# Gathered blocks as one run of 17 tiles, and one block multiplied with its counts as stationary operand

## The chip, the cores and the metric

The kernel runs on one core of one Trainium2 chip. The metric is the device time of one launch in microseconds, as the median over runs. One further execution was profiled; all rows of the profile come from it.

## The reference

Four layers of a graph network over 6250 nodes of 256 channels and 100,000 edges, sorted by destination (`N`, `C`, `E`; `NOUT` is 64):

```python
def agg(h):
    return jax.ops.segment_sum(h[src], dst, num_segments=N)
x = jnp.maximum(_layernorm(x_in), 0.0)
for l in range(3):
    h = x + agg(x)
    h = relu(h @ W1s[l] + b1s[l])
    h = relu(h @ W2s[l] + b2s[l])
    x = h @ W3s[l] + b3s[l]
h = x + agg(x)
h = relu(h @ cW1 + cb1)
h = relu(h @ cW2 + cb2)
return x_in + h @ cW3 + cb3
```

Edges are drawn at random: a block of 128 destination nodes has about 2050 of them.

## The kernel before, in words

The 6250 nodes are 49 blocks of 128. The first matrix of each layer is applied ahead of the aggregation, so a layer's table holds rows that only have to be summed. A table stands in DRAM (`tables`) and, split into a high and a low half, in SBUF (`XY`, 512 columns for each of 49 source blocks).

A block's sum over its edges is made in one of two ways.

- **Dense, in panels.** In layer 0 a matrix of edge counts is built for some blocks by matmuls of one-hot matrices (`build`, lines 1016 to 1056; its one-hots `hi` and `lo` come from VectorE, line 997) and stored as bytes in DRAM (`mats`). A panel is up to four such blocks. For each of 49 source blocks (a *unit*), the counts are cast to a ring tile `a` (`prepare`, lines 1500 and 1502), and four matmuls with `XY` as stationary operand and the counts as moving operand add to two PSUM tiles (`product`, line 1527). The result has channels on partitions, as the following layers of the network want it.
- **Gathered.** Rows of the table are fetched by indirect DMAs on GpSimd, 128 rows of 1 KB each (`Gathered.send`, line 1345, a *gather*), and added by matmuls with one-hot matrices (`one_hots`, line 1370; `add`, line 1389), 32 destination nodes to one quarter of PSUM's partitions. The result has nodes on partitions; it is turned by transposes (line 1427).

Before the change 18 blocks are gathered (22 in layer 0, where the panel of blocks 44 to 47 isn't built in time), in 18 tiles each: nine for each half of the block (`TS = 9`, `T = 18`). The other 31 (27) are dense: seven panels of four blocks and one, the first, of three (blocks 17 to 19).

The order of instructions on each engine is written out by the program. `tick` counts units, and jobs are put between them; a model clock (`passed`, with the costs of line 1456) says how far PE should be. A gathered block is added in two *visits*, each to a part of its tiles, between two units; `meets` says when. `flow` sends gathers evenly over a layer, `LEAD` (21 us on the model clock) ahead of their visit. A gather waits for the matmul behind which it was sent (`after`), and for a free buffer (24 in layer 0, 26 later). A layer's gathers begin when the whole table of the layer before is stored (`begin`). The second and third product of each group of blocks (`mlp`, lines 1198 and 1255; in the last layer 1190 and 1210) follow some units later.

Layer 0 is opened by `PRE` ticks, in which counts are built and no product runs: all steps of the first panel and eight more, two a tick. The preparation ahead of it (`look`, `normed`) finds where each block's edges begin, fetches them, makes the gather indices `idx` and each edge's destination in its block (`rel`), and judges whether the edges fit the tiles (`wrong`); where they don't, a second program (`any_edges`) does all again.

Of the kernel before, what the change touches and what calls it, by code (L numbers as in the profile page):

```python
# [8 lines left out]
F32 = mybir.dt.float32  # L9
# [8 lines left out]
P = 128  # L18
# [378 lines left out]
def sorted_edges(  # L397
# [57 lines left out]
    TS = 9  # L455
    T = 2 * TS
    CUT = (3, 5)

    ROUNDS = [(3, 3), (4, 4), (0, 5), (1, 6), (2, 7), (None, 8)]
# [10 lines left out]
    gone = [(0, 4), (4, 4), (8, 4), (12, 4), (16, 1), (44, 4), (48, 1)]  # L470
    panels = [(17, 3), (20, 4), (24, 4), (28, 4), (32, 4), (36, 4), (40, 4), (44, 4)]
    S0 = 2 * panels[0][0]
    assert gone[-2] == panels[-1] and sorted(
# [16 lines left out]
    rel = const.tile([P, left[NQ]], F32, name="rel")  # L490
# [4 lines left out]
    wrong = const.tile([P, 4], F32, name="wrong")  # L495
# [4 lines left out]
    mats = [dram.tile([P, NT // CH, n, CH * P], U8, name=f"mat{p}") for p, (_, n) in enumerate(panels)]  # L500
# [108 lines left out]
    def look(pool):  # L609
# [23 lines left out]
        nc.vector.memset(one, 1.0)  # L633
        firsts = pool.tile([1, EB], F32, name="near", bufs=1)
# [26 lines left out]
        for q, (b, _) in enumerate(gone):  # L661
            nc.gpsimd.iota(place_i[:, q, :], pattern=[[1, PW]], base=T * b, channel_multiplier=-TS)
        place = pool.tile([P, 1], F32, name="place", bufs=1)
# [29 lines left out]
        for q in range(GSUB):  # L693
            for w, e in ((wd, dst), (ws, src)):
# [4 lines left out]
        both = pool.tile([P, 2], F32, name="both", bufs=1)  # L699
        sel = pool.tile([P, NQ, PW], F32, name="near_i", bufs=1)  # L700
        some = pool.tile([P, NQ, PW], F32, name="rel", bufs=1)
        nc.vector.tensor_copy(both[:NSUB, 0:1], first[:NSUB, 0:1])
        nc.vector.tensor_copy(both[:NSUB, 1:2], low[:NSUB])
        nc.vector.tensor_scalar(some[:NSUB], place_i[:NSUB], float(TS - 1), None, op0=OP.is_le)
        nc.vector.scalar_tensor_tensor(sel[:NSUB], place_i[:NSUB], 0.0, some[:NSUB],
                                       op0=OP.is_ge, op1=OP.mult)
        ps = ps_m.tile([P, W], F32, name="ps")
        for q in range(NQ):
            nc.tensor.matmul(ps[:PW, 2 * q:2 * q + 2], sel[:NSUB, q, :], both[:NSUB, :],
                             start=True, stop=True)  # L710
        spread = pool.tile([P, NQ, 2], F32, name="spread", bufs=1)
        nc.vector.tensor_copy(spread[:PW], ps[:PW, :2 * NQ].rearrange("p (q t) -> p q t", t=2))
# [25 lines left out]
        for q0 in range(0, GSUB, H):  # L738
# [42 lines left out]
        nc.vector.tensor_scalar(size[:NSUB, 0:1], less[:NSUB, GSUB:], less[:NSUB, 0:1],  # L781
                                float(TS * P), op0=OP.subtract, op1=OP.is_gt)
        nc.vector.tensor_scalar(size[:NSUB, 1:2], less[:NSUB, Q // GD:Q // GD + 1],
                                less[:NSUB, 0:1], float(CUT[1] * P), op0=OP.subtract, op1=OP.is_gt)
        nc.vector.tensor_scalar(size[:NSUB, 2:3], less[:NSUB, Q // GD:Q // GD + 1],
                                less[:NSUB, 0:1], float(CUT[0] * P), op0=OP.subtract, op1=OP.is_lt)
        nc.vector.tensor_reduce(wrong[:NSUB, 3:4], size[:NSUB, 0:3], axis=mybir.AxisListType.X,
                                op=OP.max)
# [10 lines left out]
        for t, o in ((fd, rel), (fs, idx)):  # L799
            ps = ps_m.tile([P, W], F32, name="ps")  # L800
            for q, (_, n) in enumerate(gone):
                nc.tensor.transpose(ps[:, left[q]:left[q + 1]], t[:n * T, q, :],
                                    ident[:n * T, :n * T])
            if o is rel:
                nc.vector.tensor_scalar(o, ps[:, :left[NQ]], -1.0, None, op0=OP.add)
            else:
                nc.vector.tensor_copy(o, ps[:, :left[NQ]])
# [3 lines left out]
    def verdict():  # L811
        bad = ps_m.tile([P, W], F32, name="ps")
        nc.tensor.matmul(bad[:1, :4], one, wrong, start=True, stop=True)
        return bad

    def judge(bad):
        nc.vector.tensor_reduce(amiss, bad[:1, :4], axis=mybir.AxisListType.X, op=OP.add)
# [108 lines left out]
    with tc.manual_schedule():  # L926
# [38 lines left out]
        def load_weights(l):  # L965
# [4 lines left out]
            else:  # L970
                w3 = late.tile([2 * NOUT, C], F32, name="cw3", bufs=1)
                for h in range(2):
                    nc.sync.dma_start(out=w3[h * NOUT:(h + 1) * NOUT, :], in_=cW3)
                row = late.tile([P, C], F32, name="cb3r", bufs=1)
# [6 lines left out]
        batches = [(p, s, q0) for p, (b0, n) in enumerate(panels)  # L981
# [34 lines left out]
        def build(hots, ats, ps_b):  # L1016
# [7 lines left out]
            for k, (p, s, q0) in enumerate(batches):  # L1024
                i, half = divmod(s - 2 * panels[p][0], 2)
# [5 lines left out]
                for q in range(0, BATCH, 2):  # L1031
# [17 lines left out]
                    if half and q0 + q + 2 == GSUB:  # L1049
                        own = at[:, panels[p][0] + i, :]  # L1050
# [9 lines left out]
        def first_chunks(i, at):  # L1060

            n = panels[0][1]
            if i == n - 1:
                for k, chunk in enumerate(opening):
# [3 lines left out]
                        chunk[:, :n, j * P:(j + 1) * P] for j in range(CH))  # L1068
# [8 lines left out]
        def fetch(l, p):  # L1077

            n = panels[p][1]
            c = len(mat.setdefault((l, p), [])) // CH  # L1080
            at = chunks.tile([P, 4, CH * P], U8, name="at", bufs=5)
            nc.sync.dma_start(out=at[:, :n, :], in_=mats[p][:, c, :, :])
            mat[l, p].extend(at[:, :n, j * P:(j + 1) * P] for j in range(CH))
# [216 lines left out]
        class Gathered:  # L1300
            def __init__(self, l):
# [4 lines left out]
                               if l == 0 or (b, n) != panels[-1]]  # L1306
                self.alone = {b + i for b, n, i, _ in self.blocks}
                self.visits = [(g, rounds) for g in range(len(self.blocks)) for rounds in VISITS[l > 0]]
# [3 lines left out]
                self.order = [(g, k, h) for g, rounds in self.visits for k in self.tiles(rounds)  # L1312
                              for h in range(2)]
                self.upto = [0]
                for _, rounds in self.visits:
                    self.upto.append(self.upto[-1] + 2 * len(self.tiles(rounds)))

            @staticmethod
            def tiles(rounds):
                return sorted({k for r in rounds for k in ROUNDS[r] if k is not None})  # L1320
# [18 lines left out]
            def send(self, upto):  # L1339
                while self.sent < min(upto, len(self.order)):  # L1340
                    g, k, h = self.order[self.sent]
                    t = gath.tile([P, C], F32, name="rows")
                    self.rows[g, h, k] = t
                    o = self.blocks[g][3] + h * TS + k
# [16 lines left out]
            def one_hots(self, v):  # L1361
                g, rounds = self.visits[v]
                o = self.blocks[g][3]
                self.hots = {}
                for r in rounds:
                    hot = work.tile([P, 2, 2, Q], F32, name="hot", bufs=6)
                    for i, k in enumerate(ROUNDS[r]):
                        if k is not None:
                            self.hots[r, i] = hot[:, i, :, :]
                            nc.vector.tensor_tensor(  # L1370
                                hot[:, i, :, :],
                                colf[:, None, i * Q:(i + 1) * Q].to_broadcast([P, 2, Q]),
                                rel[:, o + k:o + k + TS + 1:TS, None].to_broadcast([P, 2, Q]),
                                OP.is_equal)

            def add(self):
# [3 lines left out]
                if rounds[0] == 0:  # L1380
                    self.sums = sums
                if v == 0:
                    self.one_hots(0)
                end = rounds[-1] == len(ROUNDS) - 1
                for r in rounds:
                    for h in range(2):
                        for m, k in enumerate(ROUNDS[r]):
                            if k is not None:
                                nc.tensor.matmul(  # L1389
                                    self.sums[(2 * h + m) * Q:(2 * h + m + 1) * Q, :C],  # L1390
                                    self.hots[r, m][:, h, :], self.rows[g, h, k], start=(r == 0),
# [264 lines left out]
```

## Time and profile before

| | us |
|---|---|
| median of 3 runs | 2163.5 (2163.37 to 2166.09) |
| the profiled execution: time | 2161.71 |
| the profiled execution: span | 2159.9 |
| mean granted clock of TensorE | 0.991 |

| engine | busy us | share of the span |
|---|---|---|
| PE, matmuls | 2102.0 | 97% |
| VectorE (DVE) | 987.4 | 46% |
| ScalarE (ACT) | 900.7 | 42% |
| GpSimd (POOL) | 1417.2 | 66% |

How to read it: the times of all rows are microseconds from the start of the span, except where "mean ns of one" is said. A matmul in fp32 is recorded as two instructions, one in fp32r (the products of line 1527) or bf16 (line 1038) as one. Busy time of PE is the union of its instructions' modelled spans. Layer 0 runs to about 722 us, layers 1, 2 and 3 begin there, at 1215 and at 1709.

### The profile page before, as it was taken

Reading aid. Unit: us, or ns where it says so; the run is one execution under the profiler, and the core shown is the slowest. Engines: PE = TensorE matmul, PEld = TensorE weight load, DVE = VectorE, ACT = ScalarE, POOL = GpSimd, SP = SyncE. Lnnn points to the kernel's source line nnn. Section 1 sums busy time; section 2 is a strip of 40 time slices with the busy share of each in tenths; the row PEclk is TensorE's granted clock in tenths of the full one; section 3 lists DMA queues with packets and bytes.
Section 4 is the critical chain, followed back from the end, with each engine's and each line's share of the span. In section 5 each row is a group of like instructions: output and inputs, shape, how many; then the busy total and the mean of one; then the engine's idle time right before and its main releaser. Section 6 shows DMA issues by size and latency. Waiting matters only on the chain.

```text
span 2159.9 us, 34383 instructions
## 1 busy us (share of the span) xinstructions
PE 2102.0 (97%) x12106; PEld 1553.3 (72%) x12106; DVE 987.4 (46%) x2844; ACT 900.7 (42%) x1816; POOL 1417.2 (66%) x1442
## 2 busy tenths in 40 slices
PE   5889999999999999999999999999999999999998
PEld 4657766766666877777777877777777877777775
DVE  7988666666664532222234433322333433333323
ACT  4876655556555423233324433232223433333331
POOL 3637777777775366666666366666666277777773
PEclk9979999999999999999999999999999999999999
DMA  5556656656565655544555655545555565556563
GB/s 162 167 162 198 189 177 188 188 184 195 168 212 180 199 158 154 162 142 148 157 169 178 193 159 155 160 138 163 155 171 170 158 202 183 188 168 193 191 191 110
DMA packets 195965, 371.51 MB, mean 172 GB/s; under 512 B 32808, under 2 KB 123068, under 8 KB 195782
## 3 DMA queue, kind: packets, MB, share of 16 engines
q0 software_dynamic: 67264, 181.96, 28.6%
q1 hardware_dynamic: 126590, 185.40, 26.1%
q8 instruction: 97, 1.59, 0.3%
q10 hardware_dynamic: 1928, 1.85, 0.3%
q14 instruction: 86, 0.70, 0.1%
HBM read 310.67 MB, written 58.07 MB: 171 GB/s over the span
## 4 chain that ended last, share of the span: by engine, by line
PE 91%; DVE 4%; ACT 2%; DMA 2%; issue 1%; POOL 0%; SPq 0%; ACTq 0%; DVEq 0%; POOLq 0%
PE agg L1527 62%; PE sums L1389 10%; PE ps L1198 6%; PE ps L1255 6%; PE bp L1038 4%; DVE hi L997 1%; PE ps L1427 1%; DMA back<-table 1%; PE bp L882 1%; PE ps L1210 1%; DVE lo L997 0%; PE ps L1190 0%; PE ps L578 0%; ACT at L1046 0%; DMA table<-zs 0%
## 5 line engine op out<-in xcount | busy, mean ns | idle before, releaser
L1345 POOL DMA_INDIRECT rows<-table,idx x1368 | 1362.7, 996 | 668.3 <-PE agg L1527 267.4
L1527 PE MATMUL agg<-a,XY 128*128 128x512 f32 (+1 forms) x6076 | 1455.3, 391 | 5.9 <-ACT h L1543 2.9
L1527 PEld LDWEIGHTS agg<-a,XY 128*128 128x128 f32 x6076 | 1105.2, 188 | 259.8 <-issue 51.2
L1500 ACT CAST a<-at 128x512 fp32r<-128x512 uint8 (+1 forms) x943 | 554.8, 607 | 606.1 <-PE agg L1527 581.1
L1502 DVE CAST a<-at 128x512 fp32r<-128x512 uint8 (+1 forms) x576 | 270.9, 474 | 529.0 <-PE agg L1527 496.8
L1389 PE MATMUL sums<-rows,hot 128*32 128x256 f32 x3344 | 231.3, 384 | 2.6 <-DMA rows<-table,idx 1.9
L1046 ACT CAST at<-bp 128x392 uint8<-128x392 f32 x276 | 131.0, 488 | 215.1 <-PE bp L1038 212.7
L1048 DVE CAST at<-bp 128x392 uint8<-128x392 f32 x220 | 123.8, 563 | 157.6 <-PE bp L1038 157.2
L1389 PEld LDWEIGHTS sums<-rows,hot 128*32 128x32 f32 x3344 | 103.3, 109 | 117.4 <-issue 50.6
L1038 PE MATMUL bp<-hi,lo 128*128 128x196 bf16 x992 | 133.8, 259 | 10.4 <-DVE hi L997 9.0
L1416 DVE TENSOR_TENSOR u<-u,sums 128x256 f32<-128x256 f32 x76 | 31.7, 418 | 240.6 <-PE agg L1527 240.6
L997 DVE TENSOR_TENSOR hi<-cols,pairs 128x784 bf16<-128x784 bf16 x248 | 138.3, 558 | 0.0
L1198 PE MATMUL ps<-h,w 128*128 128x512 f32 (+4 forms) x348 | 136.8, 536 | 0.0
L1255 PE MATMUL ps<-w,h 128*128 128x256 f32 x588 | 133.7, 379 | 0.0
L1038 PEld LDWEIGHTS <-lo 128*128 128x128 bf16 x992 | 73.9, 100 | 81.7 <-DVE hi L997 33.4
L1370 DVE TENSOR_TENSOR hot<-colf,rel 128x64 f32<-128x64 f32 x836 | 126.4, 216 | 0.0
L1255 PEld LDWEIGHTS ps<-w,h 128*128 128x128 f32 x588 | 110.9, 190 | 15.3
L997 DVE TENSOR_TENSOR lo<-lanes,pairs 128x512 bf16<-128x512 bf16 x248 | 103.1, 416 | 2.1 <-ACT pairs L992 1.3
L1263 DVE TENSOR_TENSOR zz<-ps,w 128x512 f32<-128x512 f32 (+1 forms) x78 | 50.4, 657 | 117.1 <-PE ps L1255 117.1
L1198 PEld LDWEIGHTS ps<-h,w 128*128 128x128 f32 (+1 forms) x348 | 62.6, 191 | 53.8 <-issue 44.3
L1201 ACT ACTIVATE h<-ps,bias 128x512 f32<-128x512 f32 (+4 forms) x87 | 53.2, 628 | 98.3 <-PE ps L1198 98.2
L1434 ACT ACTIVATE h<-ps,bias 128x256 f32<-128x256 f32 (+1 forms) x84 | 33.5, 450 | 133.2 <-PE ps L1427 133.1
(143 smaller groups left out, 743.2 us busy)
## 6 DMA issues: line engine op xcount, KB each, us to landing
at<-mat SPq DMA_DIRECT2D x189, 448.0 KB
mat<-at SPq DMA_DIRECT2D x31, 784.0 KB
rows<-table,idx POOLq DMA_INDIRECT x1368
table<-zz SPq DMA_DIRECT2D x69, 256.0 KB
back<-table SPq DMA_DIRECT2D x118, 128.0 KB
at<-mat SPq DMA_DIRECT2D x25, 336.0 KB
xs<-in_x_dram SPq DMA_DIRECT2D x8, 768.0 KB
table<-zs SPq DMA_DIRECT2D x24, 256.0 KB
```

Of the source, the lines that this page charges most:

```text
L997: nc.vector.tensor_tensor(o.rearrange("p q (n t) -> p q n t", t=2), values.rearrange("p (n t) -> p n t", t=2)[:, None, :, :].to_broadcast( ...
L1038: mm = nc.tensor.matmul(bp[:, m * HW:(m + 1) * HW], lo[:, q + m, :], hi[:, q + m, :], start=True, stop=True)
L1046: nc.scalar.copy(o, v)
L1048: nc.vector.tensor_copy(o, v)
L1198: mm = nc.tensor.matmul(ps[:mp, :w], weights[l][0][:, c, i * P:i * P + mp], h1[:, c, :w], start=(c == 0), stop=(c == KC - 1))
L1255: mm = nc.tensor.matmul(o, h2[0][:, c, nodes], w3[:, c, :], start=(c == 0), stop=(c == KC - 1))
L1345: got = nc.gpsimd.indirect_dma_start(out=t, out_offset=None, in_=tables[self.l][:, :], in_offset=bass.IndirectOffsetOnAxis(ap=idx[:, o:o + ...
L1370: nc.vector.tensor_tensor(hot[:, i, :, :], colf[:, None, i * Q:(i + 1) * Q].to_broadcast([P, 2, Q]), rel[:, o + k:o + k + TS + 1:TS, None] ...
L1389: nc.tensor.matmul(self.sums[(2 * h + m) * Q:(2 * h + m + 1) * Q, :C], self.hots[r, m][:, h, :], self.rows[g, h, k], start=(r == 0), stop= ...
L1500: nc.scalar.copy(o, mat[l, p][j])
L1502: nc.vector.tensor_copy(o, mat[l, p][j])
L1527: mm = nc.tensor.matmul(agg[c][:, :w], XY[:, j, o:o + P], a[:, :w], start=(j == 0 and half == 0), stop=(j == NT - 1 and half == 1))
```

## The change

A gathered block becomes one run of 17 tiles (`T = 17`), without halves. Quarter m of the block's nodes may have its edges in tiles 4m - 1 to 4m + 4, and the matmuls go in rounds of one tile for each quarter, 23 in place of 22. The one-hots of a visit are made by one VectorE operation of 128x384, in place of five or six of 128x64. Where the quarters' edges must end is judged by four bounds (`CUTS`).

Blocks 16 to 18 are now gathered in each layer: 20 blocks (25 in layer 0, block 19 among them). Block 19 is `solo` in layers 1 to 3: its counts are built and stored as before, but multiplied as the stationary operand, with 512 columns of `XY` as moving operand, 49 matmuls in place of a share of panel matmuls; the sum of its two halves is then turned together with block 18. It comes after three panels. Seven panels of four blocks are left (six in layer 0), and counts are built for 29 blocks in place of 31. The opening has 36 ticks in place of 28, since the first panel has four blocks. The last layer's small tiles are put where the build's inputs were, and the later gather pool has 27 buffers.

The core of the diff:

```diff
-    TS = 9
-    T = 2 * TS
-    CUT = (3, 5)
-
-    ROUNDS = [(3, 3), (4, 4), (0, 5), (1, 6), (2, 7), (None, 8)]
+    T = 17
+    CUTS = ((3, 5), (7, 9), (11, 13), (0, T))
+    ROUNDS = ((3, 1, -1), (0, 4, 2))
...
-    gone = [(0, 4), (4, 4), (8, 4), (12, 4), (16, 1), (44, 4), (48, 1)]
-    panels = [(17, 3), (20, 4), (24, 4), (28, 4), (32, 4), (36, 4), (40, 4), (44, 4)]
+    gone = [(0, 4), (4, 4), (8, 4), (12, 4), (16, 4), (44, 4), (48, 1)]
+    panels = [(20, 4), (24, 4), (28, 4), (32, 4), (36, 4), (40, 4), (44, 4)]
+    solo = (19, 1)
+    stock = panels + [solo]
...
             def one_hots(self, v):
                 g, rounds = self.visits[v]
...
-                for r in rounds:
-                    hot = work.tile([P, 2, 2, Q], F32, name="hot", bufs=6)
-                    for i, k in enumerate(ROUNDS[r]):
-                        if k is not None:
-                            self.hots[r, i] = hot[:, i, :, :]
-                            nc.vector.tensor_tensor(
...
+                shape = [P, len(rounds), P // Q, Q]
+                self.hot = work.tile(shape, F32, name="hot", bufs=2)
+                nc.vector.tensor_tensor(
+                    self.hot,
+                    colf.rearrange("p (m q) -> p m q", q=Q)[:, None, :, :].to_broadcast(shape),
+                    rel[:, self.blocks[g][3] // T, v % len(ROUNDS), :, :, None].to_broadcast(shape),
+                    OP.is_equal)
...
+                for c in rounds:
+                    for m in range(P // Q):
+                        if c + 4 * m >= 0:
+                            nc.tensor.matmul(
+                                self.sums[m * Q:(m + 1) * Q, :C],
+                                self.hot[:, (c - min(rounds)) // 2, m, :], self.rows[g, c + 4 * m],
+                                start=(c == ROUNDS[0][0]), stop=(c == ROUNDS[-1][-1]))
...
+        def product_by_node(l, ps_a):
+            agg = ps_a.tile([P, W], F32, name="agg")
+            for j0, m in solo_parts:
+                u = now[0]
+                tick(layers[l])
+                layers[l].advance()
+                prepare(u + 1 + AHEAD + 2)
+                a = ring.pop(u)
+                for j in range(j0, j0 + m):
+                    mm = nc.tensor.matmul(agg, a[:, (j - j0) * P:(j - j0 + 1) * P], XY[:, j, :],
+                                          start=(j == 0), stop=(j == NT - 1))
+                    passed(W * COLS, mm)
+            u = spare[:, :C]
+
+            def halves():
+                nc.scalar.copy(u, agg[:, :C])
+                later(1, lambda: nc.vector.tensor_tensor(u, u, agg[:, C:], OP.add))
+
+            later(1, halves)
+            alone[l] = u
...
-        gath = ctx.enter_context(tc.tile_pool(name="gath2", bufs=26))
+        gath = ctx.enter_context(tc.tile_pool(name="gath2", bufs=27))
```

More of the change, by code (lines that the diff above doesn't have):

```diff
@@ L1379, in add @@
                 b, n, i, _ = self.blocks[g]
-                if rounds[0] == 0:
-                    self.sums = sums
+                self.sums = sums
                 if v == 0:
                     self.one_hots(0)
[L1384 to L1391, printed above, removed]
-                                    stop=(r == (len(ROUNDS) - 2 if m == 0 else len(ROUNDS) - 1)))
+                end = rounds == ROUNDS[-1]
+                for c in rounds:
+                    for m in range(P // Q):
[4 more added lines that the diff above has]
+                                start=(c == ROUNDS[0][0]), stop=(c == ROUNDS[-1][-1]))
                 passed(VISIT)
@@ L1458, in sorted_edges @@
         FAR, SPAN = 7, 6
-        ends = [PRE + NT * sum(k + 1 for k in last[:l + 1]) for l in range(NLAYER + 1)]
-        VISITS = [[[0, 1, 2], [3, 4, 5]], [[0, 1, 2], [3, 4, 5]]]
+        ends = [sum(1 for k, *_ in units if k <= l) for l in range(NLAYER + 1)]
         layers = [Gathered(l) for l in range(NLAYER + 1)]
@@ L1465, in work_of @@
         def work_of(l):
-            t = sum(n for _, n in panels[:last[l] + 1]) * P * NT * 2 * KC * COLS
-            t += len(layers[l].blocks) * (sum(VISIT for _ in VISITS[l > 0]) + TURN)
+            t = sum(stock[p][1] for p in order[l]) * P * NT * 2 * KC * COLS
+            t += len(layers[l].blocks) * (len(ROUNDS) * VISIT + TURN)
             for k, n in ((l, NT - panels[last[l]][1]), (l - 1, panels[-1][1])):
@@ L1547, in sorted_edges @@
         load_weights(0)
-        total = GSUB * sum(n for _, n in panels)
+        total = GSUB * sum(n for _, n in stock)
         built, goals = [0], []
```

173 lines of the change are left out of this document (106 added, 67 removed).

## The prediction

> **What bounds the kernel now.** I read the page first: its engine shares, then its chain of waits.
>
> ```profile
> PE 2102.0 (97%) x12106; PEld 1553.3 (72%) x12106; DVE 987.4 (46%) x2844; ACT 900.7 (42%) x1816; POOL 1417.2 (66%) x1442
> ...
> PE 91%; DVE 4%; ACT 2%; DMA 2%; issue 1%; POOL 0%; SPq 0%; ACTq 0%; DVEq 0%; POOLq 0%
> ```
>
> By these rows PE is the bound and POOL has a third of its time free. The change takes work from PE and gives some to POOL, so I looked at POOL's gathers alone: the groups by line in three stretches, inside layer 0 (160 to 650 us), layer 1 (740 to 1180) and layer 3 (1740 to 2130). After the bar stand busy us and mean ns of one, then the idle time before them.
>
> ```profile
> L1345 POOL DMA_INDIRECT rows<-table,idx x355 | 369.9, 1042 | 120.9 <-issue 61.9 <-PE bp L1038 29.3 <-PE agg L1527 23.8
> ...
> L1345 POOL DMA_INDIRECT rows<-table,idx x309 | 299.7, 970 | 141.4 <-PE agg L1527 86.2 <-issue 36.6 <-PE ps L1255 9.4
> ...
> L1345 POOL DMA_INDIRECT rows<-table,idx x302 | 298.4, 988 | 93.2 <-issue 46.6 <-PE agg L1527 39.2 <-DMA rows<-table,idx 3.7
> ```
>
> The timeline shows POOL at both ends of layer 3, and PE's last visit (a visit is one of the two halves in which a gathered block is summed):
>
> ```profile
> 1712.88 0.95 POOL L1345 DMA_INDIRECT rows<-table,idx  x1 [33.74 <-DMA cw<-in_L_gnn_cW_dram]
> ...
> 2128.03 0.96 POOL L1345 DMA_INDIRECT rows<-table,idx  x1 [0.30 <-issue]
> ...
> 2131.03 0.95 POOL L1345 DMA_INDIRECT rows<-table,idx  x1 [0.30 <-DMA rows<-table,idx]
> ...
> 2132.80 1.60 PE L1389 MATMUL sums<-rows,hot 128*32 128x256 f32 x20
> ```
>
> In layer 3 a gather takes 298.4 / 302 = 0.988 us and is preceded by 93.2 / 302 = 0.309 us of idle time. The 0.30 stands even before a gather that waits for nothing ("issue"), so it is part of the price: 1.297 us each, and POOL never rests there. The page counts that 0.30 as idle, which is how a saturated engine shows 66%. The last gather ends at 2131.98 and the visit that needs it starts 0.8 us later. So layer 3 already has two bounds of one length. In layer 0 a gather costs 1.042 + 0.30 = 1.342 against a spacing of (369.9 + 120.9) / 355 = 1.383: 3% of slack. At that layer's end it is gone, and PE stands until rows land:
>
> ```profile
> 685.44 0.95 POOL L1345 DMA_INDIRECT rows<-table,idx  x1 [0.30 <-DMA rows<-table,idx]
> ...
> 688.24 0.62 PE L1389 MATMUL sums<-rows,hot 128*32 128x256 f32 x2 [0.66 <-DMA rows<-table,idx]
> ```
>
> Layer 1 has room: 0.970 + 0.30 = 1.270 against (299.7 + 141.4) / 309 = 1.427; layer 2 is built like it.
>
> The Trainium skill, Perfetto Trace Analysis, section GPSIMD Engine Instruction, advises timing this engine by start-to-start spacing, not by reported spans. That is what the sum of the two columns does.
>
> **PE's part.** Prices come from the chain of waits in undisturbed stretches, and from the groups by form.
>
> ```profile
> 1215.21 21.50 PE agg L1527 x124
> ...
> 798.48 12.03 PE agg L1527 x52
> 810.51 1.43 PE sums L1389 x20
> ...
> 947.49 3.43 PE ps L1198 x8
> 950.92 1.43 PE sums L1389 x24
> ...
> 963.96 3.45 PE ps L1255 x16
> ```
> ```profile
> L1038 PE MATMUL bp<-hi,lo 128*128 128x196 bf16 x992 | 133.8, 259 | 10.4 <-DVE hi L997 9.0 <-ACT at L1046 0.6
> ...
> L1427 PE MATMUL ps<-ident,u 128*128 128x128 f32 x152 | 23.5, 272 | 0.6 <-DVE zz L1239 0.6
> ```
>
> Removed in each of four layers: the panel of three blocks, 196 matmuls 384 wide at 21.50 / 124 = 0.173, 34.0 us. Added in layers 1 to 3: the solo block, 49 matmuls 512 wide at 12.03 / 52 = 0.231, 11.3 us. No row shows counts as stationary operand; the shape is that of the 512-wide products, and a doubled price (22.7) is the other end. Added: three gathered blocks in layer 0, two in each other layer. A block has 23 matmuls (46 recorded) instead of 22, still in two visits; visits of 20 and of 24 recorded ones both take 1.43, so a block costs 2.86, plus two transposes of 23.5 / 152 = 0.155: 3.2 us. Builds fall from 31 blocks to 29: 64 matmuls of 133.8 / 992 = 0.135, 8.6 us, all in layer 0.
>
> The opening, which builds the first panel's counts before any product, grows from 56 steps to 72. Its window:
>
> ```profile
> 118.30:145.10 26.80, 19.92 (x114) 10.64 (x113) 24.44 (x59) 23.57 (x61) 8.69 (x8) 0.66 0.54 170
> ```
>
> Columns are length, then busy us of PE, PEld, DVE, ACT and POOL. It runs at DVE's pace (24.44 of 26.80), so 16 steps more cost 16 × 26.80 / 56 = 7.7 us. The new preparation has some ten small DVE operations more near its end; I give them 1 us.
>
> PE alone: layer 0, -34.0 + 9.6 - 8.6 + 7.7 + 1 = -24; layers 1 to 3, -34.0 + 11.3 + 6.4 + 0.3 (the solo's transposes) = -16.0 each. Together -72.
>
> **POOL's part.** Gathers go from 396 to 425 in layer 0 and from 324 to 340 in the others: 1445 against 1368. Each waits in POOL's order, and the visit behind it holds PE's whole queue, so late rows stop the dense products too. Asking earlier does not help an engine that never rests.
>
> Layer 0: of 425 gathers the planner places 12 in the opening (8 before). The first gather behind it was here:
>
> ```profile
> 147.47 0.95 POOL L1345 DMA_INDIRECT rows<-table,idx  x1 [18.34 <-PE agg L1527]
> ```
>
> It moves by 8.7 us to 156.2. Then 413 × 1.342 = 554 us: the last ends at 710, against 686.4. PE alone would finish this layer at about 689 - 24 = 665, so rows set the end: +24 us.
>
> Layers 1 and 2 run from first gather to last visit:
>
> ```profile
> 727.02 0.95 POOL L1345 DMA_INDIRECT rows<-table,idx  x1 [40.62 <-DMA at<-mat]
> ...
> 1219.05 0.95 POOL L1345 DMA_INDIRECT rows<-table,idx  x1 [32.15 <-DMA w<-in_L_gnn_W2s_dram]
> ```
> ```profile
> 1191.33 1.50 PE L1389 MATMUL sums<-rows,hot 128*32 128x256 f32 x20
> ```
>
> That is 464.3 us. The cycle of 492 loses 16.0 on PE; of its rest, about 8 us of PE work moves behind the last visit, where four blocks (16 to 19) must now pass the second and third product instead of one (3.43 + 3.45, less a quarter of that) and the next layer's first products are 512 wide. The stretch becomes 464 - 24 = 440, and POOL needs 340 × 1.270 = 432, or 441 at layer 3's 1.297. The two meet; I take -15 a layer.
>
> Layer 3: 340 × 1.297 = 441, plus 1 until the last visit, against 2132.80 - 1712.88 = 419.9: +22, where PE alone would have 396. The tail behind it loses about 1. The step from layer 0 to 1 gains 2 (its first products are wider).
>
> **At nothing** stand the edits that other work hides.
>
> ```profile
> L1500 ACT CAST a<-at 128x512 fp32r<-128x512 uint8 (+1 forms) x943 | 554.8, 607 | 606.1 <-PE agg L1527 581.1
> ...
> DMA packets 195965, 371.51 MB, mean 172 GB/s; under 512 B 32808, under 2 KB 123068, under 8 KB 195782
> ...
> at<-mat SPq DMA_DIRECT2D x25, 336.0 KB
> ```
>
> ACT's 943 casts for the products fall to 830; it waits for PE in nearly all the idle time ahead of them, so fewer bring nothing. The solo's sum leaves PSUM by one ACT copy and one DVE addition in each of three layers; block 18, which takes it along into the transposes, ends more than half a layer later. If that cover failed, it would be about 1 us a layer. On SP's queue the 28 chunk loads of the narrow panel go and six of the solo's come; with 77 more gathers of 131 KB, and two blocks fewer to build and store, the 371 MB stay within 1%. The last layer's two small weight loads go to a tile that the builds have left free; SP issues them at the same place. The longer order of one-hots per visit is DVE's, and DVE has half its time free behind the opening.
>
> **Sum.** +24 + 2 - 15 - 15 + 22 - 1 = +17 us. The profiled execution has a span of 2159.9 and a time of 2161.7; 2161.7 + 17 = 2178.7. The median of the three runs, 2163.5, is 1.8 above it, which would make 2180.5; I forecast 2179.
>
> **What is unknown** is a gather's price. In layer 0 it swells beside DVE operations that read two SBUF tiles:
>
> ```profile
> 670.47 0.41 DVE L1407 TENSOR_TENSOR u<-XY 128x256 f32<-128x256 f32 x1
> 670.54 1.99 POOL L1345 DMA_INDIRECT rows<-table,idx  x1 [0.30 <-issue]
> 670.81 0.41 DVE L997 TENSOR_TENSOR lo<-lanes,pairs 128x512 bf16<-128x512 bf16 x1
> 671.14 0.55 DVE L997 TENSOR_TENSOR hi<-cols,pairs 128x784 bf16<-128x784 bf16 x1
> ...
> L997 DVE TENSOR_TENSOR hi<-cols,pairs 128x784 bf16<-128x784 bf16 x201 | 112.1, 558 | 0.0
> ...
> L1370 DVE TENSOR_TENSOR hot<-colf,rel 128x64 f32<-128x64 f32 x836 | 126.4, 216 | 0.0
> ```
>
> The change makes the one-hots of a block (11 of 216 ns) into two wide ones, 128x384, whose duration I put between the 216 and the 558 ns of these rows' kinds. They read the same two tiles as the old ones (`rel` now in bf16), so I count no new stall. The other end: layer 0's surplus over layer 1, 355 × (1.042 - 0.970) = 25.6 us, charged to the 201 one-hots `hi` in that stretch, is 0.13 us each; 90 such in layers 0 and 3 are +12, and 80 in layers 1 and 2 +10. Low end: half the surplus of layer 0 (-15) and layer 1's 1.270 in layer 3 (-9).
>
> The Trainium skill, SBUF — State Buffer, section Who interferes with whom, infers that a tensor_tensor does not stall descriptor generation, while a cast in a two-port mode does. In layer 0 only ACT makes the casts `a<-at`, and gathers are longest there, beside tensor_tensors; the trace speaks against the inference. By that rule the wide one-hots would add 0, as in my sum.
>
> **The rivals.** First, PE stays the bound and the kernel gets faster: -72, so 2163.5 - 72 = 2091. It needs the 0.30 before each gather to vanish with demand; it decides below about (665 - 157 - 2) / 413 = 1.22 us a gather in layer 0 and 395 / 340 = 1.16 in layer 3. For it: PE's 97%. Against: 302 gathers in a row at 1.297. Chance 0.07. The Trainium skill, DMA: Bandwidth & Descriptors, section Anatomy of one DMA, calls descriptor generation small until many are emitted; by that rule the extra gathers are nearly free and this rival holds. The rows above deny it.
>
> Second, the wide one-hots stall gathers as `hi` does: +22 on the forecast, 2201. For it: the 1.99 us gather. Chance 0.14.
>
> Third, gain and loss cancel: POOL's price falls by 17 / 753 = 0.023 us over layers 0 and 3, because fewer builds disturb it; 2163. Chance 0.10.
>
> Fourth, the kernel's own verdict finds a block beyond 17 tiles, and the second program runs as well: its some 829 gathers in each of four layers at 1.25 are over 4,100 us more. Counted over the reference's destinations, the fullest gathered block has 2130 edges, 17 tiles hold 2176, and the quarter marks lie inside their bounds. Chance 0.01.
>
> **How the numbers follow.** The forecast has 0.68. The range takes the low end of the price, 2179 - 24, rounded down for the solo and the boundaries, and the high end with 5 us beyond: 2152 to 2206; it leaves out the first and the fourth rival. 0.2% (4.3 us) is about what a measurement of this kernel can tell from no change. Faster by more: the first rival and a third of the third, 0.10; within: 0.07; slower: 0.83.
>
> **What would show it.** Right: in the profile after, layers 0 and 3 have gathers with 0.30 idle before nearly each, PE idle ahead of `sums` put down to DMA rows, some 45 us in layer 0 and 45 in layer 3, and PE's share down to about 93%; the last gather of layer 0 near 710. The solo's 147 products take 34 us. Wrong: a spacing of gathers below 1.22 us in layer 0, or visits that never wait while the time falls.

## The result, and the profile after

The changed kernel took 2179.1 us (median of four runs, 2175.6 to 2180.9) against 2164.0 before: 1.0066 times as long, 95% interval 1.0049 to 1.0083. Forecast were 2179 and "slower". The profiled execution has a span of 2179.1 us, 19.2 more than before, while the medians are 15.1 apart: a profile is one execution, and can lie some us off the median.

The first view is again the page's engine shares (busy us, share of the span, instructions).

```profile
PE 2068.1 (95%) x11971; PEld 1467.6 (67%) x11971; DVE 907.2 (42%) x2108; ACT 843.8 (39%) x1682; POOL 1492.8 (69%) x1521
```

PE has 34 us less to do and the span is 19 us longer. POOL still looks a third idle. The groups by line say why that is wrong; they are the gathers of the same three stretches as in the prediction (160 to 650 us, 740 to 1180, 1740 to 2130).

```profile
L1377 POOL DMA_INDIRECT rows<-table,idx x368 | 370.3, 1006 | 120.7 <-issue 60.3 <-PE bp L1068 25.2 <-PE agg L1586 22.3
...
L1377 POOL DMA_INDIRECT rows<-table,idx x328 | 324.0, 988 | 144.8 <-issue 59.1 <-DMA back<-table 43.4 <-PE agg L1586 33.8
...
L1377 POOL DMA_INDIRECT rows<-table,idx x303 | 298.7, 986 | 92.4 <-issue 49.4 <-PE agg L1586 29.9 <-DMA rows<-table,idx 8.5
```

In layer 3 a gather has 92.4 / 303 = 0.305 us of idle time ahead of it. In layer 1 it has (144.8 - 43.4) / 327 = 0.310, once the 43.4 us before the layer's first gather are left out; it was 0.458 before. So POOL now runs without a rest in layer 1 too. In layer 0 the mean, 0.328, still holds the opening. The timeline shows where each layer's gathers begin, and the last ones.

```profile
137.17 1.05 POOL L1377 DMA_INDIRECT rows<-table,idx  x1 [0.30 <-issue]
151.74 1.35 POOL L1377 DMA_INDIRECT rows<-table,idx  x1 [13.52 <-PE bp L1068]
...
165.75 0.95 POOL L1377 DMA_INDIRECT rows<-table,idx  x1 [2.71 <-PE agg L1586]
...
710.76 0.95 POOL L1377 DMA_INDIRECT rows<-table,idx  x1 [0.30 <-issue]
...
755.06 1.44 POOL L1377 DMA_INDIRECT rows<-table,idx  x1 [43.36 <-DMA back<-table]
...
1234.49 1.03 POOL L1377 DMA_INDIRECT rows<-table,idx  x1 [38.62 <-PE agg L1586]
...
1714.38 1.02 POOL L1377 DMA_INDIRECT rows<-table,idx  x1 [38.48 <-PE agg L1586]
...
2152.39 0.95 POOL L1377 DMA_INDIRECT rows<-table,idx  x1 [0.30 <-issue]
```

Layer 0's last gather starts at 710.8; "near 710" was forecast. Cut at the first gather of each layer, the two spans compare like this:

| us | before | after | difference | forecast |
|---|---|---|---|---|
| start to layer 1's first gather | 727.0 | 755.1 | +28.0 | +26 |
| to layer 2's | 492.0 | 479.4 | -12.6 | -15 |
| to layer 3's | 493.8 | 479.9 | -13.9 | -15 |
| to the end | 447.0 | 464.7 | +17.7 | +21 |

What PE lost is in the row of its visits, in layers 0, 1 and 3 (160 to 715 us, 755 to 1200, 1714 to 2160):

```profile
L1414 PE MATMUL sums<-rows,hot 128*32 128x256 f32 x1150 | 93.2, 394 | 29.4 <-DMA rows<-table,idx 28.5 <-DVE hot L1397 0.6 <-DVE u L1441 0.3
...
L1414 PE MATMUL sums<-rows,hot 128*32 128x256 f32 x920 | 60.7, 383 | 0.8 <-DMA rows<-table,idx 0.8
...
L1414 PE MATMUL sums<-rows,hot 128*32 128x256 f32 x920 | 77.6, 387 | 22.3 <-DMA rows<-table,idx 21.9
```

Idle time tells only half of it. The 920 visit matmuls of layer 3 are "busy" for 77.6 us and the same 920 of layer 1 for 60.7: part of the wait for rows is drawn as busy time inside a visit. So layer 3 loses 22.3 + 16.9 = 39 us to rows. Layer 0 loses 29.4 + (93.2 - 60.7 x 1150 / 920) = 47. The visits show it one by one (start, duration, idle time before):

```profile
711.10 1.08 PE L1414 MATMUL sums<-rows,hot 128*32 128x256 f32 x8 [2.00 <-DMA rows<-table,idx]
713.58 1.91 PE L1414 MATMUL sums<-rows,hot 128*32 128x256 f32 x10 [1.40 <-DMA rows<-table,idx]
...
2155.22 1.05 PE L1414 MATMUL sums<-rows,hot 128*32 128x256 f32 x10 [1.29 <-DMA rows<-table,idx]
```

### The profile page after: what moved, and what is told of

Same layout as the page of the kernel before. It is cut to its first block, busy times and chain, and to the rows that moved or that the text cites. A ratio compares the mean times of both kernels' runs of the same rounds, so it can differ in the third digit from the quotient of the medians.

```text
span 2179.1 us, 33141 instructions
## 1 busy us (share of the span) xinstructions
PE 2068.1 (95%) x11971; PEld 1467.6 (67%) x11971; DVE 907.2 (42%) x2108; ACT 843.8 (39%) x1682; POOL 1492.8 (69%) x1521
## 5 line engine op out<-in xcount | busy, mean ns | idle before, releaser
L1377 POOL DMA_INDIRECT rows<-table,idx x1445 | 1435.4, 993 | 610.7 <-issue 242.6
L1586 PE MATMUL agg<-a,XY 128*128 128x512 f32 x5292 | 1318.0, 400 | 4.3 <-ACT h L1602 2.2
L1586 PEld LDWEIGHTS agg<-a,XY 128*128 128x128 f32 x5292 | 973.2, 189 | 259.4 <-issue 54.3
L1538 ACT CAST a<-at 128x512 fp32r<-128x512 uint8 (+1 forms) x830 | 499.2, 619 | 608.4 <-PE agg L1586 562.6
L1538 DVE CAST a<-at 128x512 fp32r<-128x512 uint8 (+1 forms) x535 | 240.4, 451 | 554.2 <-PE agg L1586 487.9
L1414 PE MATMUL sums<-rows,hot 128*32 128x256 f32 x3910 | 292.4, 387 | 53.2 <-DMA rows<-table,idx 51.9
L1414 PEld LDWEIGHTS sums<-rows,hot 128*32 128x32 f32 x3910 | 121.9, 109 | 206.3 <-DMA rows<-table,idx 86.9
L1231 PE MATMUL ps<-h,w 128*128 128x512 f32 (+2 forms) x316 | 133.4, 564 | 0.0
L1397 DVE TENSOR_TENSOR hot<-colf,rel 128x384 f32<-128x384 f32 x170 | 93.4, 551 | 0.0
L1234 ACT ACTIVATE h<-ps,bias 128x512 f32<-128x512 f32 (+2 forms) x79 | 50.8, 659 | 84.5 <-PE ps L1231 84.5
```

Source lines behind the costliest of these rows:

```text
L1231: mm = nc.tensor.matmul(ps[:mp, :w], weights[l][0][:, c, i * P:i * P + mp], h1[:, c, :w], start=(c == 0), stop=(c == KC - 1))
L1234: later(soon, lambda: nc.scalar.activation(h2[0][:mp, i, :w], ps[:mp, :w], AF.Relu, bias=b2[l][:mp, i:i + 1]))
L1377: got = nc.gpsimd.indirect_dma_start(out=t, out_offset=None, in_=tables[self.l][:, :], in_offset=bass.IndirectOffsetOnAxis(ap=idx[:, o:o + ...
L1397: nc.vector.tensor_tensor(self.hot, colf.rearrange("p (m q) -> p m q", q=Q)[:, None, :, :].to_broadcast(shape), rel[:, self.blocks[g][3] / ...
L1414: nc.tensor.matmul(self.sums[m * Q:(m + 1) * Q, :C], self.hot[:, (c - min(rounds)) // 2, m, :], self.rows[g, c + 4 * m], start=(c == ROUND ...
L1538: cast(o, at[:, :, d:d + m * P])
```

## Experiments

The theory: POOL, at about 1.3 us a gather with its 0.30 of idle time, sets the time of layers 0 and 3 and just about that of layers 1 and 2. The rivals: PE is the bound and the gathers are hidden; the wide one-hots stall the gathers.

The runs met chips of two kinds. Beside e1 to e4 and e9 to e11 the median of the kernel before was 2163 to 2164 us, as in the first comparison; beside e5 to e8 and e12 it was 2323 to 2326. Times are compared within one kind only.

| run | us | ratio to the kernel before, beside it |
|---|---|---|
| e1, one gather less | 2115.3 | 0.9775 [0.9758, 0.9791] |
| e2, two gathers less | 2087.6 | 0.9653 [0.9634, 0.9672] |
| e3, one gather more | 2281.0 | 1.0547 [1.0530, 1.0565] |
| e4, narrow one-hots | 2193.5 | 1.0145 [1.0128, 1.0162] |
| e5, early visits | 2418.6 | 1.0409 [1.0389, 1.0429] |
| e6, two by node | 2412.7 | 1.0377 [1.0360, 1.0395] |
| e7, and layer 0 | 2389.1 | 1.0261 [1.0231, 1.0291] |
| e8, balanced | 2379.7 | 1.0235 [1.0216, 1.0254] |
| e9, changed again | 2176.5 | 1.0046 [1.0025, 1.0067] |
| e10, balanced again | 2136.2 | 0.9863 [0.9843, 0.9883] |
| e11, casts on ACT | 2128.1 | 0.9826 [0.9804, 0.9848] |
| e12, ring moved | 2382.3 | 1.0251 [1.0228, 1.0274] |

### e1, e2, e3: fewer and more gathers, the same work on PE

In `send`, e1 (`N = 16`) and e2 (`N = 15`) leave gathers out, e3 makes one twice:

```diff
                     g, k = self.order[self.sent]
+                    if k >= N:                        # e1, e2
+                        self.rows[g, k] = self.rows[g, k - 2]
+                        self.sent += 1
+                        continue
...
+                    if k == 4 and (g, T) not in self.rows:    # e3
+                        self.rows[g, T] = self.rows[g, 4]
+                        continue
                     self.sent += 1
```

> One gather of each block is left out, its last tile; its matmuls read the rows of another tile instead, so PE, DVE and ACT have the same instructions in the same order, and the sums lack the edges of that tile. POOL as the bound: layer 0 loses 25 gathers of 1.31 us (-33 us), layer 3 loses 20 of 1.29 (-26); in layers 1 and 2 PE takes over at once, -4 each: about -67 us, 2112. PE as the bound, gathers hidden: no change, 2179.

> Two gathers of each block are left out in the same way. POOL as the bound: POOL alone would give -65 us in layer 0 and -52 in layer 3, but PE takes over before that, when its waits for rows are gone: the 47 us that visits lose to rows in layer 0 of the changed kernel, and 39 in layer 3; layers 1 and 2 -4 each. About -94 us, 2085, which is the time that PE alone would need (the prediction's first rival, 2091). The step from one gather less to two is smaller than the first step. PE as the bound now: no change, 2179.

> One gather of each block is made twice, and one matmul reads the second copy; PE, DVE and ACT have the same instructions in the same order. POOL as the bound, or just at it, in all four layers: +25 gathers of 1.31 us in layer 0 (+33) and +20 of 1.29 in each of the others (+26 each): +111 us, 2290. If layers 1 and 2 had more slack than the few us that the trace shows, up to 20 us less. PE as the bound: no change.

Measured were 2115, 2088 and 2281 against 2112, 2085 and 2290. PE's instructions are the same in all of them, so its work cannot be what set the time. The first gather left out brings 64 us and the second 28: the curve bends where PE takes over. From the profiles, layer 0 (to layer 1's first gather) goes from 755 to 720 and then 706, the stretch from layer 3's first gather to the end from 465 to 440 and 423. Layers 1 and 2 give 1 to 2 us each, where 4 were expected: PE's own cycle there is 478. In e3 layers 1 to 3 add 23.6, 24.0 and 24.2, near the 26 expected of a POOL that is the bound in each of them, and layer 0 only 23.5 of the 33. Its timeline gives the rest: the first gather came 2.1 us earlier, POOL stood 3.5 us less, a gather took 1.008 us in place of 1.013 (2.5 us in all), and the step to layer 1 was 1.4 shorter. The gathers of e3 in layer 3 (1800 to 2230 us), then the visits of layer 3 in e2 (1660 to 2060):

```profile
L1377 POOL DMA_INDIRECT rows<-table,idx x335 | 329.0, 982 | 102.1 <-issue 59.1 <-PE agg L1589 29.0 <-DMA rows<-table,idx 8.5
```
```profile
L1418 PE MATMUL sums<-rows,hot 128*32 128x256 f32 x896 | 58.6, 383 | 0.0
```

In e3 the price is the same, 0.982 + 0.305 = 1.287, however many gathers there are. In e2 the visits of layer 3 wait for nothing (those of layer 0 for 3.8 us), and the 2088 us it needs are near what the prediction's first rival gave for PE alone (2091): the sum of PE's part was right, but it was not the one that counted.

Leaving gathers out also leaves out their transfers. These were not the limit: in layer 3 of the changed kernel, where rows come late, the DMA engines were busy for 0.57 of the time and moved 178 GB/s; in e2, where none is late, it was 0.58 and 183 (the last two numbers of each row):

```profile
1740.00:2130.00 390.00, 370.43 (x2193) 262.99 (x2192) 118.46 (x260) 105.46 (x189) 297.94 (x303) 0.99 0.57 178
```
```profile
1680.00:2040.00 360.00, 358.78 (x2235) 262.08 (x2234) 120.13 (x265) 107.30 (x191) 273.76 (x278) 1.00 0.58 183
```

### e4: narrow one-hots

```diff
-                nc.vector.tensor_tensor(
-                    self.hot,
...
+                for r in range(len(rounds)):
+                    for i in (0, 2):
+                        nc.vector.tensor_tensor(
+                            self.hot[:, r, i:i + 2, :],
```

> The wide one-hot operation of a visit (128x384) is made by six of 128x64 again, everything else is as in the changed kernel. My theory: the wide ones stall gathers no more than the small ones did, so the time stays within 5 us of 2179. The second rival: each of the 170 wide ones costs a gather 0.13 us that the small ones don't, so the time falls by about 22 us, to 2157, and the mean gather of layer 3 falls from 0.986 us towards 0.953.

It came out on neither side: 2193.5, some 14 us slower than the changed kernel. The gathers from 200 to 700 us and from 1740 to 2130, first in the changed kernel, then in e4:

```profile
L1377 POOL DMA_INDIRECT rows<-table,idx x382 | 385.4, 1009 | 116.4 <-issue 62.2 <-PE agg L1586 19.8 <-PE bp L1068 18.9
...
L1377 POOL DMA_INDIRECT rows<-table,idx x303 | 298.7, 986 | 92.4 <-issue 49.4 <-PE agg L1586 29.9 <-DMA rows<-table,idx 8.5
```
```profile
L1377 POOL DMA_INDIRECT rows<-table,idx x371 | 388.2, 1046 | 113.1 <-issue 66.7 <-PE bp L1068 19.5 <-PE agg L1588 13.7
...
L1377 POOL DMA_INDIRECT rows<-table,idx x305 | 298.4, 978 | 92.9 <-issue 45.7 <-PE agg L1588 34.7 <-DMA rows<-table,idx 7.0
```

In layer 0 the narrow operations make a gather 0.037 us longer, which is the price of the kernel before again (1.042 in the prediction's row). That is 0.037 x 413 = 15 us; in the profiles layer 1's first gather comes 9.7 us later (764.8 for 755.1). In layer 3 they make it 0.008 shorter, 3 us. So the wide form was worth some 10 to 15 us in layer 0, where DVE also builds `hi` and `lo`. The timelines show where: 28 gathers of e4's stretch began while `u` or a narrow one-hot was under way, and took 1.41 us on average; in the changed kernel 27 began under `u` or a wide one-hot, and took 1.10 (how this is counted stands in the last section).

### e5 to e8, e9 and e10: taking work from POOL

e5 lets layer 0's visits begin earlier:

```diff
-                self.first = clock[0] + LEAD
+                self.first = clock[0] + (LEAD if self.l else 8.0)
```

> Only layer 0's first visit is put earlier, 8 us on the model clock behind the start in place of 21, so that gathers run on through the opening, where POOL stands still for 13.5 us and waits for `bp` behind it; the pace over the layer is stretched to match. POOL as the bound of layer 0: some 16 gathers more are done when the first product starts, 16 x 1.31 = -21 us, 2158. If what holds layer 0 back is PE or DVE in the opening, nothing is gained, or a few us are lost by the visits put between the builds.

e6 and e7 say for each layer which blocks are multiplied by node, and build block 18's counts too (e7 builds block 19's ahead of the last two panels'):

```diff
-    solo = (19, 1)
-    stock = panels + [solo]
+    solos = [(19, 1), (18, 1)]
+    ALONE = {0: (), 1: (19,), 2: (19,), 3: (18, 19)}        # e7: 0: (19,)
+    stock = panels + solos
...
-                               if l == 0 or (b, n) != panels[-1] and b + i != solo[0]]
+                               if (l == 0 or (b, n) != panels[-1]) and b + i not in ALONE[l]]
```

> In layer 3 block 18 is multiplied with its counts as stationary operand too, so 19 blocks are gathered there in place of 20; its counts are built in layer 0 (16 steps more). POOL as the bound: layer 3 loses 17 gathers of 1.29 us (-22), PE gets 11.6 - 3.2 = 8 us more, which fits into the 39 us that its visits lose to rows; layer 0 and the others stay: 2157. PE as the bound: +8 in layer 3 and about +4 in layer 0, 2191.

> As the run before, and block 19 is multiplied by node in layer 0 too, behind four panels, its counts built ahead of the last two panels': 24 blocks are gathered there in place of 25. POOL as the bound: -22 us more in layer 0, where PE's new 8 us fit into the 47 that visits lose to rows: 2135. PE as the bound: +8 instead.

> All three together: the visits of layer 0 begin early, 24 blocks gathered in layer 0 and 19 in layer 3. POOL of layer 0 by itself -22 - 21 = -43, but PE alone ends that layer about 47 - 8 - 4 = 35 us earlier than now, so -35 there and -22 in layer 3: 2122, below both kernels. If early visits gain nothing, 2135.

None of the expected times can be compared with what was measured, because these chips run every kernel longer. Only the differences are left: 17 gathers less in layer 0 (e6 to e7) brought 23.6 us where 22 were expected, early visits on top of that (e7 to e8) 9.5 where 13 were. So the balanced kernel was run once more, beside the changed one.

> The changed kernel as it is, as the measure for the two runs beside it and for the four before, whose chip ran the kernel before in 2326 us. On a chip like the first: 2179. On one like that of the last four, those runs leave 2437: there the run with two blocks by node lost 17 gathers of 1.46 us (25) and came to 2413, the one with early visits to 2419.

> The balanced kernel beside the changed one: POOL as the bound gives -35 us in layer 0 and -22 in layer 3 against the changed kernel on a chip like the first, 2122, which is below the kernel before too; on a chip like that of the last four, where gathers come every 1.46 us, -57 as well (2380 against 2437), and above the kernel before.

These runs met a chip like the first. The changed kernel took 2176.5 and the balanced one 2136.2, below the kernel before by 1.4% and by 40 us below the changed one. 57 were expected. The visits of its layer 0 (160 to 680 us) now hardly wait:

```profile
L1414 PE MATMUL sums<-rows,hot 128*32 128x256 f32 x1082 | 72.9, 386 | 3.6 <-DMA rows<-table,idx 3.6
```

By layers, from the two profiles: -37.2 to layer 1's first gather and -21.4 behind layer 3's, as expected (-35, -22); the two profiles are 47.7 apart, the medians 40.3. But layers 1 and 2 became 5.0 and 5.9 us longer, and there PE waits for nothing. The dense matmuls themselves are slower, first in the changed kernel (e9), then in the balanced one (e10; both 800 to 1150 us):

```profile
L1586 PE MATMUL agg<-a,XY 128*128 128x512 f32 x996 | 235.7, 394 | 0.0
```
```profile
L1601 PE MATMUL agg<-a,XY 128*128 128x512 f32 x974 | 235.4, 399 | 0.0
```

Some 1,300 such matmuls a layer by 0.0045 us are the 6 us. e12 follows this up.

### e11: all casts on ACT

```diff
-                cast = nc.scalar.copy if l == 0 or ready[0] % 2 == 0 else nc.vector.tensor_copy
+                cast = nc.scalar.copy
```

> The balanced kernel with all casts `a<-at` of layers 1 to 3 on ACT (535 of them are DVE's in the changed kernel). Gathers of layer 3 that a DVE cast alone overlaps took 0.984 us in place of 0.953, so if the casts stall them, the mean falls from 0.987 by up to 0.02 us: -7 us in layer 3, up to -5 in each of layers 1 and 2, about -12 against the balanced kernel. If ACT cannot keep up (0.62 us for each cast of a 0.92 us unit, and its other work), PE waits for casts and the kernel gets slower, by up to 20 us.

8 us less than the balanced kernel, of 12 expected. Gathers of layer 1 (800 to 1150 us), balanced and then with the casts moved:

```profile
L1377 POOL DMA_INDIRECT rows<-table,idx x267 | 261.4, 979 | 89.9 <-issue 41.4 <-PE agg L1601 39.7 <-PE ps L1231 3.5
```
```profile
L1377 POOL DMA_INDIRECT rows<-table,idx x268 | 255.7, 954 | 96.1 <-PE agg L1601 45.1 <-issue 41.8 <-PE ps L1231 3.7
```

0.954 is what a gather takes alone. The surplus of layer 1 was DVE's casts and the one-hots that they moved: the one-hots are still there, but one gather of the layer begins under one of them, where 11 did in the balanced kernel. The layer itself gains only 1.1 us, because PE is its bound by now; its gathers rest a little more. Layer 3, where POOL is the bound, gains 3.1: its gathers still take 0.969 us (1740 to 2080 us), after 0.979. Layer 0, which the edit leaves alone, came out 1.4 shorter; so much do two profiles differ.

### e12: the ring of `a` moved

```diff
         late = ctx.enter_context(tc.tile_pool(name="late", bufs=1))
+        late.tile([P, 96], F32, name="pad", bufs=1)
```

> The kernel of the run before (balanced, all casts on ACT) with 384 unused bytes of each partition ahead of the ring tiles `a` of layers 1 to 3; nothing else changes. In the balanced kernels the dense matmuls of these layers start every 0.236 us on average (median 0.232), in the kernel before and the changed one every 0.231 (0.227), without a wait between; the ring lay 128 bytes elsewhere there (288 in place of 160 modulo 512). If its place is the cause, the pitch is 0.231 again: 1,300 matmuls a layer by 0.0045 = -6 us in each of layers 1 and 2, where PE sets the time, and nothing in layer 3, where POOL does: 2116, 0.977 of the kernel before. If it is not, 2128, 0.983.

It met a chip of the slower kind, so the time says nothing about the 12 us. The pitch can still be read where nothing disturbs it: undisturbed rows of 44 dense matmuls on the timeline, of the changed kernel (e9), of the balanced one (e10) and of this one:

```profile
841.79 10.28 PE L1586 MATMUL agg<-a,XY 128*128 128x512 f32 x44
```
```profile
873.00 10.50 PE L1601 MATMUL agg<-a,XY 128*128 128x512 f32 x44
```
```profile
1020.32 10.28 PE L1601 MATMUL agg<-a,XY 128*128 128x512 f32 x44
```

10.28, 10.50, 10.28: with the ring back at its old place modulo 512 bytes, the old pitch is back (the median from start to start is 0.227, 0.232 and 0.227 us). Neither the kind of chip nor the casts explain it: the median is 0.227 in e5 too, on the slower kind of chip with the ring at its old place, and 0.232 in e6 to e8, on that kind, and in e11, with all casts on ACT, where the ring has the new place. The place of the moving operand is the cause. That the kernel then takes 2116 us was not measured.

## Why the prediction was right, point by point

**POOL as the bound.** Shown, by e1 to e3: PE's instructions were the same, and the DMA engines had time left. The 0.30 us ahead of each gather does not shrink with demand: the price in layer 3 was 1.297 forecast, 0.986 + 0.305 = 1.291 measured.

**Layer 0, +24.** The last gather came at 710.8 for "710", but by two errors that cancelled, which is luck. First, the preparation grew by 9 us and not by 1: the opening's builds start at 127.39, where they started at 118.29. DVE's rows before and after show where:

```profile
11.83 0.42 DVE L841 BATCH_NORM_STATS2 stats<-xs 128x6 f32<-128x256 f32 x1
...
110.42 0.57 DVE L805 TENSOR_SCALAR rel<-ps 128x396 f32<-128x396 f32 x1 [1.14 <-PE ps L802]
111.36 0.57 DVE L807 CAST idx<-ps 128x396 int32<-128x396 f32 x1 [0.37 <-PE ps L802]
...
113.45 0.69 DVE L894 COPY zs<-bp 128x512 f32<-128x512 f32 x1 [0.93 <-PE bp L882]
```
```profile
15.89 0.15 DVE L666 TENSOR_SCALAR halves<-halves 128x1 int32<-128x1 int32 x1 [3.58 <-POOL halves L665]
...
16.21 0.42 DVE L871 BATCH_NORM_STATS2 stats<-xs 128x6 f32<-128x256 f32 x1
...
117.50 1.08 DVE L834 TENSOR_SCALAR rel<-ps 128x100 bf16<-128x100 f32 x6 [3.03 <-PE ps L827]
...
122.55 0.69 DVE L924 COPY zs<-bp 128x512 f32<-128x512 f32 x1 [2.76 <-PE bp L912]
```

The prediction priced DVE's new operations and not the waits that came with them. DVE now waits 3.6 us for POOL before the statistics, which begin 4.4 us later, and near the end 5.8 us for PE in place of 2.4; 1.3 us is left for the operations themselves, where 1 was forecast. (In e1 to e4, which prepare in the same way, the first gather came 6.6 to 7.4 us later than before, and here 9.1.) The opening itself was sized well, 35.6 us long for 26.8 + 7.7 (its window, with the granted clock as the last but two of the numbers):

```profile
127.39:163.03 35.64, 29.14 (x144) 15.30 (x144) 32.16 (x76) 31.07 (x79) 13.15 (x12) 0.52 0.53 171
```

So the gathers came late: the first one behind the opening began at 165.75 and not at 156.2, and POOL still waited for PE now and then up to 177. Second, "I count no new stall" for the wide one-hots was mis-sized: e4 shows that they took 0.037 us off each gather of this layer. The price behind the opening was (385.4 + 116.4) / 382 = 1.314 in place of 1.342, 0.028 x 413 = 12 us less.

**Layers 1 and 2, -15 each.** -12.6 and -13.9. "The two meet" held: PE alone needs 478 us for the cycle (e1, e2), and POOL's gathers made it 479.4 and 479.9.

**Layer 3, +22, and the tail, -1.** Together +17.7. From first gather to the start of the last, 438.0 us, where 440 were forecast; the stretch behind it got 2 us shorter. The four stretches sum to +19.2 where +17 was forecast; that the median met 2179 to the microsecond is luck as well.

**PE's part, -72.** e2 took 2088 us with PE as the bound; 2091 was the forecast of that rival. The solo's price, its one unmeasured term, was that of the 512-wide products, as taken:

```profile
L1551 PE MATMUL agg<-XY,a 128*128 128x512 f32 x147 | 34.9, 393 | 0.0
```

**The signs.** "Some 45 us" of rows in layer 0 and in layer 3 are 47 and 39, but "PE idle ahead of `sums`" shows only 29 and 22 of them, and PE's share fell to 95% and not to 93%: a visit that waits between its matmuls is drawn as busy. That sign was named too plainly.

**At nothing.** The fewer casts, the solo's sum and the loads brought nothing that the profile shows. One edit that stood there did count, the form of the one-hots.

**The rivals.** "PE stays the bound" fell with e1. "The wide one-hots stall gathers" fell in layer 0, where e4 turned its sign round. In layers 1 to 3 the stall was there: in layer 1 the 16 gathers that began under a wide one-hot took 1.251 us, 4.8 us more in all than at 0.953, and the mean rose from 0.970 to 0.988 (740 to 1180 us); PE's own cycle of 478 us hid most of it, and in layer 3 e4 got 3 us back. The third rival's cheaper gather did come in layer 0 (0.028 us), but from the form of the one-hots: e4, with as few builds, has the old price. The late opening took up what it gave. The fourth did not come: the page counts 1445 gathers. The Trainium skill, DMA: Bandwidth & Descriptors, section Anatomy of one DMA, calls descriptor generation small until many descriptors are emitted; here 85 gathers more cost 102 us (e3).

## What to carry to other kernels

Time an engine that issues by its spacing from start to start, and ask whether that spacing ever gets longer: a saturated POOL is shown here as 69% busy. Work that leaves the engine with the largest share can make a kernel slower when each piece adds a little to one that has no rest, and the exchange rate decides: a block by gathers costs 17 x 1.3 = 22 us of POOL and 3 of PE, by node 12 of PE and none of POOL. Where two engines are this close, set the split for each layer by itself (e10: 24, 20, 20 and 19 blocks), and test a bound by changing its load alone.

## What the runs showed of the hardware beyond that

**Chips differ.** On the chips of e5 to e8 and e12 POOL stops every few gathers, here for 2.01 us. In 307 gathers of e12's layer 1 (830 to 1280 us) it stops 36 times for more than 1 us, for up to 2.7, and in 305 of e10's (750 to 1150) 6 times, for up to 1.3. Most rows put this down to PE (e12's timeline):

```profile
1400.49 0.95 POOL L1377 DMA_INDIRECT rows<-table,idx  x1 [0.31 <-issue]
1403.45 0.95 POOL L1377 DMA_INDIRECT rows<-table,idx  x1 [2.01 <-PE agg L1601]
1404.71 0.95 POOL L1377 DMA_INDIRECT rows<-table,idx  x1 [0.31 <-issue]
```

The gathers of the balanced kernel's layer 1, on such a chip (830 to 1280 us) and on one of the first kind (750 to 1150):

```profile
L1377 POOL DMA_INDIRECT rows<-table,idx x308 | 303.9, 987 | 147.0 <-issue 66.7 <-PE agg L1601 39.7 <-remote 19.2
```
```profile
L1377 POOL DMA_INDIRECT rows<-table,idx x306 | 299.1, 977 | 102.6 <-issue 48.1 <-PE agg L1601 44.9 <-PE ps L1231 3.8
```

A spacing of (303.9 + 147.0) / 308 = 1.464 us against (299.1 + 102.6) / 306 = 1.313. A gather itself takes nearly as long (0.987 and 0.977). PE, too, has some 23 us of idle time in that stretch that no wait explains. No run tells what stops them, or whether the chip itself is the cause, and e10, 1.4% faster than the kernel before on the one kind, is 2.4% slower on the other (e8): a balance of two engines holds for the chip that it was measured on.

**What lengthens a gather.** Gathers can be sorted by the DVE operation that was under way when they began (it began before the gather and ended over 0.13 us behind the gather's start). In layer 0 of the changed kernel (200 to 700 us) those under `hi` took 1.103 us, under `lo` 1.082, under a wide one-hot 1.155; under the casts to `at`, which read PSUM, 0.953. In its layer 1 those under a cast to `a` took 1.075, under a wide one-hot 1.251, with no operation under way 0.956. In e12 DVE makes no casts to `a` at all: 19 gathers of layer 1 began under a one-hot and took 1.097, the other 321 took 0.955. The order decides: the first gather here began 0.28 us after the one-hot, the second 0.14 us before it.

```profile
1412.01 0.56 DVE L1397 TENSOR_TENSOR hot<-colf,rel 128x384 f32<-128x384 f32 x1 [7.86 <-PE agg L1601]
1412.29 1.11 POOL L1377 DMA_INDIRECT rows<-table,idx  x1 [1.59 <-PE agg L1601]
...
1424.02 0.95 POOL L1377 DMA_INDIRECT rows<-table,idx  x1 [1.82 <-PE agg L1601]
1424.16 0.55 DVE L1397 TENSOR_TENSOR hot<-colf,rel 128x384 f32<-128x384 f32 x1
```

The Trainium skill, SBUF — State Buffer, section Who interferes with whom, has a cast in a two-port mode stall descriptor generation and, as an inference, a tensor_tensor not. For the casts to `a` of layer 1 the rows agree (1.075 under one; the mean goes from 0.979 to 0.954 in e11, with the casts gone). For the tensor_tensors that make `hi`, `lo` and the one-hots from two SBUF tiles they speak against the inference.

**The place of an operand.** 128 bytes of difference in where the moving operand lies made a 512-wide matmul 2% slower (0.232 in place of 0.227 us from start to start, e10 and e12). No run tells which other places are slow.
